# A graph-attention layer on one core: attention dealt out sooner, four overflow slots, five more tiles turned by VectorE

## Chip, cores and metric

One core of a Trainium2 chip runs the whole program. The metric is the device time of one execution in microseconds; the median over the runs counts.

## What is computed

`x` is 2708 × 1024, `adj` 2708 × 2708 with about four ones in a row; all is fp32. Cut to what matters:

```python
h = maximum(layernorm(x), 0)
q = h @ W_q.T + b_q;  k = h @ W_k.T + b_k;  v = h @ W_v.T + b_v
z = scale * (q @ k.T) * adj              # zero entries become -10000
out = x + relu(softmax(z, axis=1) @ v)
```

## The kernel before

Rows are cut into 22 tiles of 128 (the last has 20 rows), sorted by their number of neighbours in two groups, tiles 0 to 7 and from 8 on. `q·k` is computed as `(h·M)·h` with M made from W_q and W_k, so a row's scores are products of its q row with the h rows of its neighbours only. For each tile and each neighbour ("slot") GpSimd gathers 128 rows of h from `h_dram` by an indirect DMA (L610), and VectorE makes one score of 128 rows in one instruction (L863, with the tile's q rows in `pq`). Exponentials and their normalization follow (`weights`, L872 to L911; for the tiles 7 and 20, which have rows without neighbours, L893 to L902), and one weighted sum per slot into `u` (L923, L929). The sums are then multiplied by W_v.

The matrix products go in 20 "units" of two tiles. Units 0 to 9 make q (tiles 0 and 1, 2 and 3, and so on to 18 and 19), units 10 to 19 make the output of two tiles of attention in the order below; the single tile 8 comes last.

```python
order = [6, 5, 4, 3, 2, 0, 20, 7, 17, 13, 18, 12, 19, 11, 15, 10, 14, 1, 16, 9, 8]
```

A unit is a Strassen-Winograd product of seven blocks, each of eight matmul records (L1010): s2, a12, s4, s3, then the first two blocks of the next unit (a11 and s1, `opened`), then a22. The four corners of a unit's result are taken from the banks by c11, c12, c22 and c21; c22 of a late q unit is VectorE's addition at L1091 that reads the bank `psy` directly, into which the last block a22 then accumulates. c21 of a q unit is ScalarE's copy at L1099, after which SP stores the finished q rows (L1084): those of tiles from 8 on into `q_late`. When the attention reaches such a tile, SP loads its rows from `q_late` into `pq` (L833).

A tile's rows must be turned before they are operands. Either TensorE turns eight 128 × 128 pieces through the bank `pt` (L415), or the tile is "faced": ScalarE copies `u` in another order to `v` (L944), stores it in `u_dram`, SP loads it by quarters (`by_quarters`, L700, tile `or`), and VectorE turns 32 × 32 pieces (`faces`, L705). Each unit's operands are made by `upper()` (a11, a12) and `lower()` (a22, s1, s2, s3, s4), called in the unit before at steps 0 and 2. Ten tiles are faced before.

VectorE executes in the order in which the program is written from unit 4 on; the other engines' order is planned. A unit has seven places for VectorE's work, `after(0)` to `after(6)`: s2 comes after `after(1)`, c12 after `after(3)`, c22 after `after(4)`, a22 after `after(5)`. The attention is a generator, `attention(order)`, whose steps are dealt out there: `advance(share)` takes so many steps that their assumed cost, 1.3 us for a score or a sum and 0.6 for weights, comes to the share. The share is 20.9/7, less 2.3/7 for every faced tile of the next unit, from step 2 of unit 5 on.

Two tiles, 0 and 8 (HOSTS), hold the rows with more than 8 neighbours. Slots from 8 on are put into tile 21 (SECOND), whose own 20 rows have no slots: two halves of 64 rows with 7 slots each. Its unnormalized sums go through `v_dram` and are added to the hosts' sums (L929). The attention of SECOND comes just ahead of tile 0.

W_v's four blocks replace M, and their differences replace T, which are M's, while units 9 and 10 run (L1259 loads, L1263 subtractions). Gather buffers are cleared before use, eight of them by VectorE (L1254) while the neighbours are listed and sorted. Results are added to x by an indirect DMA with accumulation on GpSimd (L1109) and put in place by an indirect scatter (L808).

Of the kernel before, what the change touches and what calls it, by code (L numbers as in the profile page):

```python
# [65 lines left out]
def tile_preln_masked_attention(  # L66
# [27 lines left out]
    SECOND = NT - 1  # L94
    HP = P // 2
    VK = K[0] - WIDE
    assert K[0] == K[EARLY] and K[SECOND] == 0 and WIDE + VK <= SLOTS
    for t in HOSTS:
# [66 lines left out]
    msq = const.tile([P, 9 + NT], FT, name="msq")  # L165
    mass = const.tile([P, 2], FT, name="mass")

# [15 lines left out]

    for t in HOSTS:
        nc.vector.memset(cap[:HP, t:t + 1], float(WIDE + VK))
    K[SECOND] = VK
# [122 lines left out]
    def follow(steps):  # L309

        for step in steps.split():
# [11 lines left out]
            elif step[0] in "hk":  # L323
                keep(first, step[0] == "h")
            elif step[0] == "+":
                owe(first)
            elif step[0] == "p":
                counted(first)
            elif step[0] == "c":
                counts(*halves[first])  # L330
            elif step[0] == "o":
                sorted_at.append(sort(*halves[first]))
            elif step[0] == "w":
                pooled.close()
                with tc.issue_after((behind if first < EARLY else products)[-1].ins):
# [298 lines left out]
    def reload(lo, hi):  # L634
# [4 lines left out]
        if hi > FULL:  # L639
            loads.append(nc.gpsimd.dma_start(ptab[:REST, FULL, SLOTS:], src[(FULL - lo) * P:, SLOTS:]))  # L640
        part = slice(HP, P) if lo >= EARLY else slice(0, HP)
        loads.append((nc.gpsimd if lo >= EARLY else nc.sync).dma_start(
            ptab[part, SECOND, 0:SLOTS + 1 - WIDE], src[0:HP, WIDE:SLOTS + 1]))
        for load in loads:
# [170 lines left out]
    def ask(t):  # L815

        g_of[t] = []
        wanted.extend((t, s) for s in range(K[t]))

    def fetch(t):  # L820
# [7 lines left out]
        if t == SECOND:  # L828
            assert EARLY in formed
            gather(tq[t][:HP], q_dram[:, :], t, SLOTS - WIDE, HP)  # L830
            nc.sync.dma_start(tq[t][HP:], q_late[:HP, :])
        elif t >= EARLY:
# [6 lines left out]
    def fill():  # L839
        while wanted and free:  # L840
            t, s = wanted.pop(0)
            g = free.pop(0)
            if s == K[t]:
                half = slice(HOSTS.index(t) * HP, (HOSTS.index(t) + 1) * HP)
                nc.gpsimd.dma_start(g[:HP], v_dram[half, :])
            else:
# [28 lines left out]
    def weights(t):  # L875
# [7 lines left out]
        if t == SECOND:  # L883
            coef = w
            with tc.issue_after(chain[-1].ins):
                chain.append(nc.vector.scalar_tensor_tensor(w[:, :k], w[:, :k], 1.0, ok, op0=ALU.mult, op1=ALU.mult,
                                                            accum_out=mass[:, 0:1]))
            nc.sync.dma_start(mass[:HP, 1:2], mass[HP:, 0:1])
            nc.scalar.activation(u, g_of[t][0], AF.Copy, scale=w[:, 0:1])
# [14 lines left out]
        else:  # L904
            with tc.issue_after(chain[-1].ins):
                nc.vector.scalar_tensor_tensor(w[:, :k], w[:, :k], 1.0, ok, op0=ALU.mult, op1=ALU.mult, accum_out=m[:, 1:2])
                if t in HOSTS:
                    second = HOSTS.index(t)
                    nc.vector.tensor_add(m[:HP, 1:2], m[:HP, 1:2], mass[:HP, second:second + 1])
                nc.vector.reciprocal(m[:, 3:4], m[:, 1:2])  # L910
                chain.append(nc.vector.tensor_scalar(coef[:, :k], w[:, :k], m[:, 3:4], None, op0=ALU.mult))  # L911
            nc.scalar.activation(u, g_of[t][0], AF.Copy, scale=coef[:, 0:1])  # L912
            free.append(g_of[t][0])
            if t in HOSTS:
                assert whole_second
                wanted.insert(0, (t, k))
        us[t] = u, coef, m

    def sums(t):
        u, coef, m = us.pop(t)  # L920
        for s in range(0 if t in EMPTY else 1, K[t]):
            fill()
            chained(lambda: nc.vector.scalar_tensor_tensor(  # L923
                u, g_of[t][s], coef[:, s:s + 1], u, op0=ALU.mult, op1=ALU.add))
            free.append(g_of[t][s])
            yield 1.3
        fill()
        if t in HOSTS:
            chained(lambda: nc.vector.scalar_tensor_tensor(  # L929
                u[:HP], g_of[t][K[t]][:HP], m[:HP, 3:4], u[:HP], op0=ALU.mult, op1=ALU.add))  # L930
            free.append(g_of[t][K[t]])
# [7 lines left out]
        unit = next((n for n, pair in enumerate(units) if pair[0] == "o" and t in pair[1:]), len(units))  # L939
        if now < [unit - 2, 2] and unit <= len(q_pairs) + 4:  # L940
            faced_tiles.add(t)
        if t in faced_tiles:
            v = row_tile(f"v_{t}")
# [15 lines left out]
    def attention(order):  # L959
# [11 lines left out]
        for i, t in enumerate(order):  # L971
            nxt = after[i]
            ahead = nxt is not None and K[t] + K[nxt] <= HIGH + 1
            part = scores(nxt, after[i + 1]) if nxt is not None else iter(())
# [38 lines left out]
    opened_of = {}  # L1013

    def opened(n):

# [6 lines left out]
        nc.scalar.copy(Y, X)  # L1023
        products.append(add_block(Z, ops["s1"], T[:, 0]))
        p5 = small("p5")
# [18 lines left out]
    def multiply(n, results, after):  # L1044
# [6 lines left out]
        after(1)  # L1051
        products.append(add_block(Y, ops["s2"], T[:, 1]))
        u2 = small("u2")
# [57 lines left out]
    def o_results(ta, tb):  # L1111
# [12 lines left out]
        def c12(Z, u2):  # L1124
            nc.vector.tensor_add(u2, Z, u2)
            nc.scalar.activation(ya[:, hi], u2, AF.Relu)
            if ta == NT - 2:

                nc.sync.dma_start(tail_dram, ya[P - 1:, :])
            send(add_x(ya, ta))  # L1130
            sent.append((ya, ta))

        def c21(Y):
            nc.scalar.activation(yb[:, lo], Y, AF.Relu)  # L1134
            send(add_x(yb, tb))
            sent.append((yb, tb))

# [29 lines left out]

    def send(behind):

        while sent:  # L1170
            y, t = sent.pop(0)
            with tc.issue_after(behind.ins):
                scatter(y, t, P)

    def tail(t):
        n = tiles[t][1]
        y = work.tile([P, D], FT, tag="q", name=f"y_{t}", bufs=4)
        nc.sync.dma_start(y[:n], tail_dram.to_broadcast([n, D]))
        add_x(y, t, n)
        scatter(y, t, n)  # L1180

# [7 lines left out]
    alone = order[-1]  # L1189
    units = [("q",) + p for p in q_pairs] + [("o",) + p for p in o_pairs]  # L1190

    def load_rows(unit):
# [17 lines left out]
    products = []  # L1210
    last_q = len(q_pairs) - 1
    summed = []
# [12 lines left out]
    for n, unit in enumerate(units):  # L1225
# [13 lines left out]
        def after(i):  # L1239
            now[1] = i  # L1240
            if (n, i) in steps_ahead:
                follow(steps_ahead[n, i])
            if (n, i) == (2, 5):
                owe(8)
                owe(9)
                rows_of[FIRST] = load_rows(units[FIRST])
                owe(10)
# [3 lines left out]
                pooled.close()  # L1251
            if (n, i) == (FIRST, 1):
                for g in slots[:HIGH - 3]:
                    nc.vector.memset(g, 0.0)  # L1254
# [109 lines left out]
    uT, (X, Z), p1 = single["turned"], single["banks"], single["first"]  # L1364
    add_block(Z, uT[:, 0:4, :], T[:, 0])
    add_block(Z, uT[:, 4:8, :], M[:, 1, 1])
# [188 lines left out]
```

## Time and profile before

| | |
|---|---|
| median of three runs | 641.19 us (641.15 to 641.2) |
| the profiled execution | 639.94 us |
| its span | 638.1 us |
| TensorE, VectorE, ScalarE, GpSimd busy | 98%, 82%, 44%, 56% |
| unit 9's first block starts | 347.10 us |
| the single tile's first block | 611.82 us |

The times of rows count from the span's start. In a timeline row stand the start, the duration, engine, line, operation, output and inputs, and in brackets the idle time before it and what ended it. In a row of the groups stand the count, the busy time, the mean duration in ns, and the idle time before the group's instructions. DMA rows end in the size and the median time to landing.

### The profile page before, as it was taken

The page shows a single profiled execution, that of the slowest core. Times are in us where ns is not written, and L with a number is a line of the kernel's source. Part 1 is how long each engine was busy: PE and PEld are TensorE (multiplying, and loading weights), DVE is VectorE, ACT ScalarE, POOL GpSimd, SP SyncE. Part 2 cuts the span into 40 slices and gives each one's busy share as a digit, 9 for nine tenths or more (in the row PEclk, how much of TensorE's full clock was granted, in tenths as well). Part 3 has the DMA queues.
Part 4 walks back from the last instruction along what each step waited for, and adds up shares of the span by engine and source line. Part 5 has one row for each costly group of instructions (what it writes and reads, how often), then busy time and mean ns, then how long its engine had stood idle before and what let it go on. Part 6 is the DMA issues. An engine that isn't in the chain of part 4 may idle for free.

```text
span 638.1 us, 6156 instructions
## 1 busy us (share of the span) xinstructions
PE 627.8 (98%) x1651; PEld 317.9 (50%) x1651; DVE 522.4 (82%) x1016; ACT 283.6 (44%) x423; POOL 360.2 (56%) x383
## 2 busy tenths in 40 slices
PE   9999999999999999999999999999999999999994
PEld 5777766444444444444444444444444444444441
DVE  5999888997997625999888999999999889989121
ACT  3538985849667533424342144343342432333200
POOL 2639960885768357565651663476466878633311
PEclk9999999999999999999999999999999999999998
DMA  8999997598796439996798998999999999853631
GB/s 335 407 362 321 342 351 286 200 323 330 255 379 231 171 95 317 327 323 223 233 299 289 290 414 222 295 344 311 363 382 325 325 290 291 266 145 77 187 119 50
DMA packets 60192, 176.96 MB, mean 277 GB/s; under 512 B 9799, under 2 KB 15255, under 8 KB 59512
## 3 DMA queue, kind: packets, MB, share of 16 engines
q0 software_dynamic: 25136, 78.41, 39.4%
q1 hardware_dynamic: 29514, 78.61, 35.0%
q10 hardware_dynamic: 5502, 19.48, 7.8%
q8 instruction: 15, 0.25, 0.2%
q14 instruction: 25, 0.20, 0.1%
HBM read 145.65 MB, written 40.74 MB: 292 GB/s over the span
## 4 chain that ended last, share of the span: by engine, by line
PE 90%; issue 4%; POOL 2%; DMA 2%; DVE 1%; POOLq 0%; ACT 0%; ACTq 0%; DVEq 0%
PE ps L1010 40%; PE psy L1010 29%; PE ps_y L476 6%; PE ps_x L476 4%; PE ps_z L476 4%; PE pt L415 4%; POOL g L610 2%; DMA v_dram<-u 1%; DMA M<-h_dram,tab 1%; PE ps_y L511 1%; DVE junk L863 0%; PE ps_h L1218 0%; PE ps_v L594 0%; DVE u L923 0%; DVE s L722 0%
## 5 line engine op out<-in xcount | busy, mean ns | idle before, releaser
L610 POOL DMA_INDIRECT g<-h_dram,tab x94 | 120.2, 1278 | 79.9 <-DVE u L923 30.0
L1010 PE MATMUL psy<-wlow,s 128*128 128x512 f32 x320 | 144.0, 592 | 0.0
L1010 PE MATMUL ps<-M,a 128*128 128x512 f32 x320 | 144.0, 593 | 0.0
L863 DVE SCALAR_TENSOR_TENSOR junk<-g,pq 128x1024 uint8<-128x1024 f32 x93 | 113.8, 1224 | 13.4 <-DMA g<-h_dram,tab 10.4
L1010 PEld LDWEIGHTS ps<-M,a 128*128 128x128 f32 x320 | 59.7, 190 | 70.4 <-issue 69.1
L923 DVE SCALAR_TENSOR_TENSOR u<-g,coef,u 128x1024 f32<-128x1024 f32 x69 | 88.4, 1281 | 7.0 <-ACT u L912 5.8
L1010 PEld LDWEIGHTS psy<-wlow,s 128*128 128x128 f32 x320 | 59.6, 190 | 69.2 <-issue 69.0
L389 DVE FIND_INDEX8 at<-ones,adj 128x8 uint32<-128x685 f32 (+1 forms) x88 | 74.5, 864 | 0.0
L1010 PE MATMUL ps<-wlow,s 128*128 128x512 f32 x160 | 72.0, 593 | 0.4 <-DVE s L722 0.4
L1010 PE MATMUL ps<-M,s 128*128 128x512 f32 x160 | 72.1, 592 | 0.0
L1010 PE MATMUL psy<-wlow,a 128*128 128x512 f32 x160 | 72.0, 593 | 0.0
L368 ACT ACTIVATE sized<-adj 128x2708 uint8<-128x2708 f32 (+1 forms) x22 | 54.3, 2467 | 7.4 <-DMA adj<-in_adj_dram 6.1
L298 POOL TENSOR_TENSOR hsum<-hsum,x 128x256 f32<-128x256 f32 (+1 forms) x56 | 38.6, 732 | 26.2 <-DVE wlow L444 22.5
L1109 POOL DMA_INDIRECT y<-in_x_dram,tab x19 | 34.2, 1798 | 28.9 <-ACT y L1134 12.1
L1010 PEld LDWEIGHTS ps<-wlow,s 128*128 128x128 f32 x160 | 30.3, 190 | 38.9 <-issue 38.5
L1010 PEld LDWEIGHTS psy<-wlow,a 128*128 128x128 f32 x160 | 30.3, 190 | 38.5 <-issue 37.3
L1010 PEld LDWEIGHTS ps<-M,s 128*128 128x128 f32 x160 | 30.3, 190 | 38.1 <-issue 37.4
L808 POOL DMA_INDIRECT out_dram<-y,tab x21 | 27.4, 1306 | 32.0 <-DMA y<-in_x_dram,tab 15.8
L912 ACT ACTIVATE u<-g,coef 128x1024 f32<-128x1024 f32 x18 | 20.7, 1149 | 35.8 <-DVE coef L911 35.6
L276 ACT ACTIVATE x<-x,r 128x1024 f32<-128x1024 f32 (+1 forms) x22 | 25.9, 1232 | 6.6 <-POOL r L266 6.6
L722 DVE TENSOR_TENSOR s<-a,pt 128x512 f32<-128x512 f32 x30 | 19.2, 681 | 10.9 <-ACT a L718 10.9
L476 PE MATMUL ps_y<-wlow 128*128 128x512 f32 x64 | 27.6, 592 | 0.0
(251 smaller groups left out, 843.3 us busy)
## 6 DMA issues: line engine op xcount, KB each, us to landing
adj<-in_adj_dram SPq DMA_DIRECT2D x21, 1354.0 KB, 11.5
x<-in_x_dram SPq DMA_DIRECT2D x21, 512.0 KB, 8.2
h_dram<-x ACTq DMA_DIRECT2D x21, 512.0 KB, 7.4
q_late<-q SPq DMA_DIRECT2D x12, 512.0 KB, 5.1
pq<-q_late SPq DMA_DIRECT2D x12, 512.0 KB, 6.6
u_dram<-v ACTq DMA_DIRECT2D x10, 512.0 KB, 6.4
or<-u_dram SPq DMA_DIRECT2D x40, 128.0 KB, 7.0
M<-in_wv_dram SPq DMA_DIRECT2D x4, 1024.0 KB, 8.4
```

What stands on the lines that cost most here:

```text
L276: nc.scalar.activation(xs[i][:n], xs[i][:n], AF.Relu, bias=r[:n, 4, i:i + 1], scale=r[:n, 3, i:i + 1])
L298: small.append(nc.gpsimd.tensor_add(hsum[:n, cols], hsum[:n, cols], xt[:n, cols]))
L368: nc.scalar.activation(sized[:n], a[:n, :, :PW], AF.Abs, accum_out=total[:n, t:t + 1])
L389: nc.vector.max_index(at[:n, k - first_k, g, :], ones[:n, 0:8], a[:n, g, :])
L415: nc.tensor.transpose(pt[:, c, :], xt[:, k * P:(k + 1) * P], ident)
L476: mm = nc.tensor.matmul(bank, a_tile(o + H * a[0], a[1], i), b(o), start=first and o == 0, stop=(o == H - 1), skip_group_check=True)
L610: return nc.gpsimd.indirect_dma_start(out=dst, out_offset=None, in_=src, in_offset=off, bounds_check=N - 1, oob_is_err=False)
L808: to = nc.gpsimd.indirect_dma_start(out=out, out_offset=bass.IndirectOffsetOnAxis(ap=ptab.bitcast(U32)[:n, t, SLOTS:SLOTS + 1], axis=0), i ...
L863: chained(lambda: nc.vector.scalar_tensor_tensor(junk, g_of[t][s], 1.0, tq[t], op0=ALU.mult, op1=ALU.mult, accum_out=zall[:, t, s:s + 1]))
L923: chained(lambda: nc.vector.scalar_tensor_tensor(u, g_of[t][s], coef[:, s:s + 1], u, op0=ALU.mult, op1=ALU.add))
L1010: mm = nc.tensor.matmul(bank, a[:, c, :], b[:, c, :], start=False, stop=(c == 3), skip_group_check=True)
L1109: return nc.gpsimd.indirect_dma_start(out=y[:n], out_offset=None, in_=x, in_offset=off, compute_op=ALU.add)
```

## The change

- **Overflow.** SECOND has 4 slots in place of 7, and the two hosts' rows are divided over its rows in pieces of 48, 8, 60 and 12; a row with more than 12 neighbours has two pieces. The second piece is added to the first by an accumulating DMA of GpSimd during the host's sums. SECOND stands ahead of tile 3 in place of tile 0.
- **Memsets and sorting.** The eight clearings go to a later place, five on VectorE, three on ScalarE; the search of the table (`searched`) is written one step sooner.
- **Dealing out.** The attention begins at step 0 of unit 5 in place of step 2, with a share of 22.0 in units up to 8, 17.4 in units 9 and 10, and 20.5 after.
- **W_v.** The block b11 and W_v's block 11 are loaded one unit step sooner, the latter into T[:, 0]; b12 − b11 goes into T[:, 1], so these two places are exchanged for the output units (`t_of`). Two subtractions stand one step later.
- **Faced tiles.** Tiles of unit 15 and of units from 19 on are faced too: 18, 12, 16, 9 and the single tile 8, which is finished and loaded at the end of unit 18 and turned in unit 19.
- **Scatters.** Each finished tile is put in place one tile later; the last tile's y lies in another buffer and goes the same way.
- The loads of the first rows of unit 4 stand ahead of two table steps, and the late put of the table waits for other instructions.

```diff
-    HP = P // 2
-    VK = K[0] - WIDE
+    VK = 4
+    OVER = ((48, 0), (8, 48)), ((60, 56), (12, 116))
...
-        wanted.extend((t, s) for s in range(K[t]))
+        wanted.extend((t, s) for s in range(K[t] + (t in HOSTS)))
...
+            if t in HOSTS and s == K[t] // 2 + 1:
+                assert len(g_of[t]) == K[t] + 1
+                rows, at = OVER[HOSTS.index(t)][1]
+                nc.gpsimd.dma_start(g_of[t][K[t]][:rows], v_dram[at:at + rows, :], accum_op=ALU.add)
...
-        if now < [unit - 2, 2] and unit <= len(q_pairs) + 4:
+        if now < [unit - 2, 2] and unit <= len(q_pairs) + 5 or unit >= len(units) - 1:
             faced_tiles.add(t)
...
-    stream = attention(order[:order.index(0)] + [SECOND] + order[order.index(0):])
+    stream = attention(order[:order.index(3)] + [SECOND] + order[order.index(3):])
...
+    def t_of(n, k):
+        return T[:, (1, 0, 2, 3)[k] if n > last_q else k]
...
-            send(add_x(ya, ta))
-            sent.append((ya, ta))
+            send(add_x(ya, ta), 1)
+            sent.append((ya, ta, P))
...
-    def send(behind):
-        while sent:
-            y, t = sent.pop(0)
+    def send(behind, stay=0):
+        while len(sent) > stay:
             with tc.issue_after(behind.ins):
-                scatter(y, t, P)
+                scatter(*sent.pop(0))
...
-        share = 20.9 / 7
+        share = (22.0 if n < last_q else 17.4 if n < last_q + 2 else 20.5) / 7
...
-            if (n, i) == (FIRST, 1):
-                for g in slots[:HIGH - 3]:
-                    nc.vector.memset(g, 0.0)
...
-            for at, place, src in (((-1, 0), b12, of_wv(0, 1)), ((0, 0), b11, of_wv(0, 0)), ((0, 2), T[:, 1], of_wv(1, 1)),
+            for at, place, src in (((-1, 0), b12, of_wv(0, 1)), ((-1, 6), b11, of_wv(0, 0)), ((-1, 6), T[:, 0], of_wv(1, 1)),
                                    ((0, 3), b21, of_wv(1, 0)), ((0, 4), b22, of_wv(1, 1))):
...
-            for at, place, a, b in (((0, 2), T[:, 0], b12, b11), ((0, 4), T[:, 1], T[:, 1], T[:, 0]),
-                                    ((1, 0), T[:, 2], b22, b12), ((1, 1), T[:, 3], b21, T[:, 1])):
+            for at, place, a, b in (((0, 2), T[:, 1], b12, b11), ((0, 4), T[:, 0], T[:, 0], T[:, 1]),
+                                    ((1, 1), T[:, 2], b22, b12), ((1, 2), T[:, 3], b21, T[:, 0])):
...
-            if n > FIRST + 1 or n == FIRST + 1 and i > 1:
+            if n > FIRST:
                 advance(share)
...
+            if (n, i) == (3, 5):
+                for g in slots[5:8]:
+                    nc.scalar.activation(g.rearrange("p (a b) -> p a b", b=P), ones.unsqueeze(1).to_broadcast([P, DC, P]),
+                                         AF.Copy, scale=0.0)
...
-            if (n, i) == (3, 4):
+            if (n, i) == (3, 3):
                 searched()
+            if (n, i) in ((3, 3), (3, 4)):
+                for g in slots[:2] if i == 3 else slots[2:5]:
+                    nc.vector.memset(g, 0.0)
...
             if nxt is None and i == 1:
+                uT = work.tile([P, D], FT, tag="hT", name="T_alone", bufs=2).rearrange("p (c q) -> p c q", q=P)
+                faces(uT, single["rows"], 0, DC)
+                single["turned"] = uT
+            if n == len(units) - 2 and i == 6:
                 while alone not in done:
                     advance(1.0)
-                r, = load_rows(("o", alone))
-                single["turned"] = turned(r, "alone")
+                single["rows"], = load_rows(("o", alone))
```

`FIRST` is 4, `EARLY` 8, `HIGH` 11, `last_q` 9, `len(q_pairs)` 10; `(n, i)` is a step i of unit n.

More of the change, by code (lines that the diff above doesn't have):

```diff
@@ L94, in tile_preln_masked_attention @@
     SECOND = NT - 1
-    HP = P // 2
-    VK = K[0] - WIDE
-    assert K[0] == K[EARLY] and K[SECOND] == 0 and WIDE + VK <= SLOTS
+    VK = 4
+    OVER = ((48, 0), (8, 48)), ((60, 56), (12, 116))
+    assert K[0] == K[EARLY] <= WIDE + 2 * VK == SLOTS and K[SECOND] == 0
+    assert sum(rows for host in OVER for rows, at in host) == P
     for t in HOSTS:
@@ L165, in tile_preln_masked_attention @@
     msq = const.tile([P, 9 + NT], FT, name="msq")
-    mass = const.tile([P, 2], FT, name="mass")
+    mass = const.tile([P, 4], FT, name="mass")
+    nc.vector.memset(mass, 0.0)
     nc.vector.tensor_copy(past, rows_i)
@@ L182, in tile_preln_masked_attention @@
         t = e
-    for t in HOSTS:
-        nc.vector.memset(cap[:HP, t:t + 1], float(WIDE + VK))
+    for t, parts in zip(HOSTS, OVER):
+        for i, (rows, at) in enumerate(parts):
+            nc.vector.memset(cap[:rows, t:t + 1], float(WIDE + (i + 1) * VK))
     K[SECOND] = VK
@@ L334, in follow @@
                 pooled.close()
-                with tc.issue_after((behind if first < EARLY else products)[-1].ins):
+                with tc.issue_after((behind if first < EARLY else rooted if first > EARLY else products)[-1].ins):
                     entered.append(put(first, int(last[0]) + 1))
@@ L640, in reload @@
             loads.append(nc.gpsimd.dma_start(ptab[:REST, FULL, SLOTS:], src[(FULL - lo) * P:, SLOTS:]))
-        part = slice(HP, P) if lo >= EARLY else slice(0, HP)
-        loads.append((nc.gpsimd if lo >= EARLY else nc.sync).dma_start(
-            ptab[part, SECOND, 0:SLOTS + 1 - WIDE], src[0:HP, WIDE:SLOTS + 1]))
+        for i, (rows, at) in enumerate(OVER[lo >= EARLY]):
+            slot = WIDE + i * VK
+            loads.append((nc.gpsimd if lo >= EARLY else nc.sync).dma_start(
+                ptab[at:at + rows, SECOND, 0:SLOTS + 1 - slot], src[0:rows, slot:SLOTS + 1]))
+            if i and lo < EARLY:
+                loads.append(nc.sync.dma_start(ptab[at:at + rows, SECOND, SLOTS - WIDE:SLOTS + 1 - WIDE],
+                                               src[0:rows, SLOTS:SLOTS + 1]))
         for load in loads:
@@ L829, in fetch @@
             assert EARLY in formed
-            gather(tq[t][:HP], q_dram[:, :], t, SLOTS - WIDE, HP)
-            nc.sync.dma_start(tq[t][HP:], q_late[:HP, :])
+            rows = sum(rows for rows, at in OVER[0])
+            gather(tq[t][:rows], q_dram[:, :], t, SLOTS - WIDE, rows)
+            for rows, at in OVER[1]:
+                nc.sync.dma_start(tq[t][at:at + rows], q_late[:rows, :])
         elif t >= EARLY:
@@ L843, in fill @@
             if s == K[t]:
-                half = slice(HOSTS.index(t) * HP, (HOSTS.index(t) + 1) * HP)
-                nc.gpsimd.dma_start(g[:HP], v_dram[half, :])
+                assert whole_second
+                rows, at = OVER[HOSTS.index(t)][0]
+                nc.gpsimd.dma_start(g[:rows], v_dram[at:at + rows, :])
             else:
@@ L907, in weights @@
                 if t in HOSTS:
-                    second = HOSTS.index(t)
-                    nc.vector.tensor_add(m[:HP, 1:2], m[:HP, 1:2], mass[:HP, second:second + 1])
+                    c, rows = HOSTS.index(t), OVER[HOSTS.index(t)][0][0]
+                    nc.vector.scalar_tensor_tensor(m[:rows, 1:2], m[:rows, 1:2], mass[:rows, c:c + 1],
+                                                   mass[:rows, c + 2:c + 3], op0=ALU.add, op1=ALU.add)
                 nc.vector.reciprocal(m[:, 3:4], m[:, 1:2])
@@ L928, in sums @@
         if t in HOSTS:
+            rows = OVER[HOSTS.index(t)][0][0]
             chained(lambda: nc.vector.scalar_tensor_tensor(
-                u[:HP], g_of[t][K[t]][:HP], m[:HP, 3:4], u[:HP], op0=ALU.mult, op1=ALU.add))
+                u[:rows], g_of[t][K[t]][:rows], m[:rows, 3:4], u[:rows], op0=ALU.mult, op1=ALU.add))
             free.append(g_of[t][K[t]])
@@ L972, in attention @@
             nxt = after[i]
-            ahead = nxt is not None and K[t] + K[nxt] <= HIGH + 1
+            ahead = nxt is not None and K[t] + (t in HOSTS) + K[nxt] <= HIGH + 1
             part = scores(nxt, after[i + 1]) if nxt is not None else iter(())
```

25 lines of the change are left out of this document (12 added, 13 removed).

## The prediction

> **What bounds the kernel now.** I read the page first: the span, the busy time of each engine and the shares of the chain that ended last. The execution took 639.94 us, its span 638.1, and the median of the three runs is 641.19; I sum on the execution and add 1.25 at the end.
>
> ```profile
> span 638.1 us, 6156 instructions
> PE 627.8 (98%) x1651; PEld 317.9 (50%) x1651; DVE 522.4 (82%) x1016; ACT 283.6 (44%) x423; POOL 360.2 (56%) x383
> PE 90%; issue 4%; POOL 2%; DMA 2%; DVE 1%; POOLq 0%; ACT 0%; ACTq 0%; DVEq 0%
> ```
>
> TensorE is busy 98% and carries 90% of the chain. Whatever leaves TensorE's work is a gain, and every moment TensorE stands still is a loss; a saving on another engine counts only if it prevents such a moment. The chain in order of time shows what a turned tile costs there.
>
> ```profile
> 472.76 0.87 PE pt L415 x8
> 473.63 6.87 PE ps L1010 x16
> ```
>
> Eight turns take 0.87 us of the chain, and sixteen product records 6.87: a block of eight is 3.43, a unit of seven blocks 24.0. Next, where TensorE waits already (timeline and waits; what stands in brackets is idle time before the row and who ended it):
>
> ```profile
> 367.06 0.68 DVE L1091 TENSOR_TENSOR q<-psy,p 128x512 f32<-128x512 f32 x1
> 367.66 1.27 DVE L923 SCALAR_TENSOR_TENSOR u<-g,coef,u 128x1024 f32<-128x1024 f32 x1
> 367.79 0.30 PEld L1010 LDWEIGHTS psy<-wlow,a 128*128 128x128 f32 x2 [0.76 <-DVE q L1091]
> 367.80 3.70 PE L1010 MATMUL psy<-wlow,a 128*128 128x512 f32 x8
> 389.03 3.67 PE L1010 MATMUL ps<-wlow,s 128*128 128x512 f32 x8 [0.36 <-DVE s L722]
> ```
>
> Both times VectorE is the last to come. At 367.8, near the end of unit 9 (the last q pair), TensorE's last block may only start when VectorE has taken the corner c22 out of the bank it accumulates in (L1091). Without that it would have started about 0.1 earlier, at 367.7. So VectorE, which executes in the written order, is just in time there, and anything that holds it up ahead of c22 of unit 9 stops TensorE at once. Small stalls today: 0.1 + 0.36 = 0.46.
>
> **The change: faced tiles.** Five more tiles (18, 12, 16, 9 and the single tile 8) are turned by VectorE. This removes 5 × 0.87 = 4.36 us from TensorE's path (8 × 109 ns each, five times). VectorE gains faces and loses nothing on its path, as the late units have idle time on it; ScalarE gains a copy and a store, SP the loads by quarters.
>
> The Trainium skill speaks against this edit (VectorE: DVE Perf Modes, sections on the three transpose paths and rules for authors): it gives TensorE 390 ns for a 128×128 turn in bf16 and says VectorE transposes only 32×32 blocks. By its 390 ns the five tiles would give 40 × 0.39 = 15.6 us and the total would be 638; the chain's 0.87 for eight in this kernel decides.
>
> Covers of the faced tiles, at nothing:
>
> ```profile
> u_dram<-v ACTq DMA_DIRECT2D x10, 512.0 KB, 6.4
> or<-u_dram SPq DMA_DIRECT2D x40, 128.0 KB, 7.0
> 586.70 1.28 DVE L929 SCALAR_TENSOR_TENSOR u<-g,m,u 64x1024 f32<-64x1024 f32 x1
> 611.82 3.60 PE L1010 MATMUL ps<-M,T_alone 128*128 128x512 f32 x8
> ```
>
> Store and load need 6.4 + 7.0, the copy some 1 to 2, the first faces 1.4: 16 to 17. Tiles 18 and 12 are finished by unit 12's first steps and their loads are written at step 4 of unit 13, tiles 16 and 9 a full unit before their first face: 20 or more each. The single tile ends at 588.0 and is used at 611.8, 24 later, so 7 are left. Without that cover each us too late would be a us of TensorE.
>
> **Four slots, memsets, scatters.** The overflow tile has 4 slots in place of 7: three scores and three sums fewer.
>
> ```profile
> L863 DVE SCALAR_TENSOR_TENSOR junk<-g,pq 128x1024 uint8<-128x1024 f32 x93 | 113.8, 1224 | 13.4 <-DMA g<-h_dram,tab 10.4
> L923 DVE SCALAR_TENSOR_TENSOR u<-g,coef,u 128x1024 f32<-128x1024 f32 x69 | 88.4, 1281 | 7.0 <-ACT u L912 5.8
> L1254 DVE MEMSET g<- 128x1024 f32 x8 | 7.3, 912 | 1.3 <-issue 1.1 <-DVE q L1094 0.2
> 235.20 0.98 POOL L612 DMA_INDIRECT pq<-q_dram,tab  x1 [4.45 <-DMA tab<-tab_dram]
> 245.75 0.95 POOL L612 DMA_INDIRECT pq<-q_dram,tab  x1 [0.30 <-issue]
> 253.19 1.22 DVE L863 SCALAR_TENSOR_TENSOR junk<-g,pq 128x1024 uint8<-128x1024 f32 x1 [1.02 <-DMA pq<-q_dram,tab]
> ```
>
> 3 × 1.224 + 3 × 1.281 = 7.5 us of VectorE, off the path. The extra small loads on SP and the accumulating transfer on GpSimd for rows of the two long tiles go with other waiting and I put them at nothing (0 to 4 us of VectorE, hidden beneath the wait found below). The eight memsets stand among the candidate listing now; half of their 7.3 us lies ahead of the index table on which GpSimd waits (235.20). Moved, and three of them given to ScalarE, the table comes about 3.7 earlier (bounds 0 and 7.3), and with it the second tile's q rows: VectorE's score of 253.19 waits for the gather of 245.75, so 3.5 earlier there too. The later scatters cost nothing: they sit on GpSimd and the last ones follow the end as before. W_v's blocks are exchanged in place and subtracted a step later; VectorE does the same four subtractions, and TensorE does not wait for them today.
>
> **Attention begins sooner and is dealt out faster: the term that decides.** Units 5 to 8 now give out 28 calls × 22/7 = 88 us of attention, against 26 × 20.9/7 = 77.6, and the overflow tile is 7.5 shorter. I went through the written order call by call. Tile 17's first score stands at step 1 of unit 10 before, and at step 0 of unit 9 after. But tile 17's q row is made by unit 8:
>
> ```profile
> 347.10 3.60 PE L1010 MATMUL psy<-wlow,s 128*128 128x512 f32 x8
> 347.66 0.57 ACT L1099 COPY q<-psy 128x512 f32<-128x512 f32 x1
> 348.25 0.33 SPq L1084 DMA_DIRECT2D q_late<-q  x1
> q_late<-q SPq DMA_DIRECT2D x12, 512.0 KB, 5.1
> pq<-q_late SPq DMA_DIRECT2D x12, 512.0 KB, 6.6
> DMA to landing us min/median/max: 3.1/5.7/11.6
> DMA to landing us min/median/max: 4.6/6.6/9.3
> 381.55 1.23 DVE L863 SCALAR_TENSOR_TENSOR junk<-g,pq 128x1024 uint8<-128x1024 f32 x1 [0.20 <-DMA pq<-q_late]
> ```
>
> Unit 8's last block ends at 347.1; ScalarE takes the last corner; SP stores the row at 348.25 and must load it again as pq of tile 17. Of the two ranges the first is of the stores, the second of the loads. With 5.1 and 6.6 the row lands at 360.0, with SP's own issue 360.2 (355.9 to 369.2 by the extremes). VectorE gets there sooner: 381.4 today, less the work that now comes behind this score (four W_v subtractions 9.1, three sides of operands, each of two faces and two operations, 8.3, c12 and c22 1.4, the bias subtraction 0.7), less 7.5 and 3.5 from above: 351. So it waits some 9 us, in order, and behind this score are written, up to c22 of unit 9: four scores (three of tile 17, one of 13), both sides of operands of unit 10 (four faces, four operations), the bias subtraction, two W_v subtractions, the weights of tile 7, its two sums, c12 and c22.
>
> ```profile
> L705 DVE STREAM_TRANSPOSE a<-or 128x512 f32<-128x512 f32 x15 | 10.0, 694 | 1.0 <-DMA or<-u_dram 1.0
> L722 DVE TENSOR_TENSOR s<-a,pt 128x512 f32<-128x512 f32 x30 | 19.2, 681 | 10.9 <-ACT a L718 10.9
> L1263 DVE TENSOR_TENSOR wlow<-M 128x2048 f32<-128x2048 f32 x2 | 4.6, 2282 | 0.0
> 371.34 0.14 DVE L894 TENSOR_SCALAR coef<-keys 128x1 f32<-128x1 f32 x1
> 373.27 0.15 DVE L902 TENSOR_TENSOR m<-w,m 128x1 f32<-128x1 f32 x1
> ```
>
> 4 × 1.224 + 4 × 0.694 + 4 × 0.681 + 0.68 + 2 × 2.282 + 2.1 (such weights, first to last row) + 2 × 1.281 + 2 × 0.68 = 21.7. Rows in a queue overlap by 0.08 (367.06 + 0.68 against 367.66), nineteen times 1.5: 20.2. The last block of unit 9 then starts at 360.2 + 20.2 = 380.4 in place of 367.7: TensorE stands still for 12.7 us (8.4 by the shortest transfers, 21.7 by the longest; I take the medians, which are many alike). It is not given back, as TensorE is the bound again afterwards. Tile 18's q row, from unit 9, meets its score in the same way one unit later, but VectorE has some 17 us written ahead of that score: 0.5 (0 to 8).
>
> By a rule of the Trainium skill (DMA: Bandwidth & Descriptors, anatomy of one DMA), about 2.0 us plus bytes over 436 GB/s, each of the two transfers would take an estimated 3.2 us, tile 17 would land at 355 and the total would be 644. The page fits that to another kind of issue; the rows here say 5.1 and 6.6.
>
> Sum: 639.94 − 4.36 − 0.46 + 12.7 + 0.5 = 648.3; with 1.25, 649.6.
>
> **Rivals.** *Same side, worse.* The attention's start doesn't move, as something other than the memsets holds the table (GpSimd's 4.45 at 235.20 is a wait for a transfer). Then VectorE runs up to 3.5 behind in units 6 to 8, whose c22 also frees TensorE's bank, and tile 17's row is made later by that: 649.6 + 3.5 = 653. For it: 10 us more work is dealt to these units. Against: the memsets do stand in the way.
> *Only a lag.* The row of tile 17 does not hold VectorE, because the score stands where the row has landed already or is fetched in another way than I read. Then VectorE at 351 needs 20.2 to c22, 371.2, and TensorE stalls 3.5: 641.19 − 4.36 − 0.46 + 3.5 = 639.9.
> *No stall.* It ends on the other side. Tile 17's first score falls behind c22 of unit 9, as it does before. From its place at step 0 to c22 there are six steps of attention; as 64 are given out in units 5 to 8, my count would have to be some six too many. Then six steps and the weights, 9.5 us, leave the queue ahead of c22, VectorE is there at 371.2 − 9.5 = 361.7, ahead of TensorE's 367.7, and the row has landed before it is wanted: 641.19 − 4.36 − 0.46 = 636.4. For it: unit 9's share is cut to 17.4 less 4.6 for its two faced tiles, and VectorE has 7.5 us less to do. Against: 5 of 7 calls of 1.83 before c22 still leave the score well ahead of it, and the q row is only stored at 348.25.
> *Not as told.* The loads of the new faced tiles come late and the turns' 4.36 go into waiting: 641.
>
> **How the numbers follow.** About 0.2%, 1.3 us, is what a measurement here can tell from no change. Forecast 0.61; worse 0.14; only a lag 0.06 (a third each faster, the same, slower); no stall 0.17; not as told 0.02 (the same). Faster 0.17 + 0.02 = 0.19; same 0.02 + 0.02 = 0.04; slower 0.61 + 0.14 + 0.02 = 0.77. The forecast's own range is 645 to 658. The range leaves out the no-stall case and the longest transfers: 639 to 657.
>
> **What would show it.** In the profile after: 15 faced tiles and 40 turns fewer; VectorE's first score near 238; a score with about 9 us of waiting for pq from q_late near 351 to 360; behind it a load of TensorE's weights of some 12 us waiting for VectorE's L1091, once. If pq waits but TensorE doesn't, my list of what is queued is wrong; if TensorE has no gap over 1 us, the whole forecast is.

## The result and the profile after

| | before | after |
|---|---|---|
| median | 641.15 us (640.8 to 641.2, 5 runs) | 655.68 us (652.93 to 656.05, 5 runs) |
| profiled execution | 639.94 us | 652.93 us |
| its span | 638.1 us | 651.0 us |

The ratio is 1.0219, with a 95% interval of 1.02 to 1.0237: slower by 2.2%. The profiled execution is the shortest of the five, so the accounts below are of 13.0 us, 639.94 to 652.93.

The page of the kernel after, the lines that answer to the first ones of the prediction:

```profile
span 651.0 us, 6123 instructions
PE 627.7 (96%) x1611; PEld 314.3 (48%) x1611; DVE 519.1 (80%) x1016; ACT 287.0 (44%) x423; POOL 361.8 (56%) x383
PE 40%; DVE 6%; issue 5%; DMA 5%; POOL 2%; ACT 1%; SPq 0%; POOLq 0%; DVEq 0%; ACTq 0%
```

The 40 turns are gone (1611 against 1651 matmuls), yet TensorE is busy as long as before: its records have become longer, as some were executed slowly after a stop. The shares of the chain can't be set beside those of before: they add up to 59%, as the chain could be followed back from the end only to 262.29 us. So I go by TensorE's waits. By cause, us in total, times, longest:

```profile
PE ps L1025 <- DVE s L729: 4.3, 1, 4.3
PE ps L1025 <- DVE a L712: 3.5, 1, 3.5
PE pt L418 <- DMA qr<-h_dram,tab: 2.2, 2, 1.6
...
PE psy L1025 <- DVE q L1109: 1.2, 1, 1.2
PE psy L1025 <- ACT u L1072: 0.8, 1, 0.8
PE ps L1025 <- ACT p L1044: 0.7, 1, 0.7
PE psy L1025 <- ACT taken L1093: 0.3, 1, 0.3
```

And its loads of weights for c22, in the same form:

```profile
PEld psy L1025 <- DVE q L1109: 2.2, 2, 2.0
```

Where the time is lost, the timeline tells. In the kernel after, unit 9's first block and unit 10's fourth (s3) start at

```profile
352.96 3.60 PE L1025 MATMUL psy<-wlow,s 128*128 128x512 f32 x8
399.64 3.60 PE L1025 MATMUL psy<-wlow,s 128*128 128x512 f32 x8
```

and in the kernel before unit 9 starts at 347.10 and that fourth block at

```profile
381.63 3.60 PE L1010 MATMUL psy<-wlow,s 128*128 128x512 f32 x8
```

Unit 9 begins 352.96 − 347.10 = 5.9 us late. At s3 of unit 10 the delay is 399.64 − 381.63 = 18.0, so units 9 and 10 lose 12.1. The end is 651.0 − 638.1 = 12.9 late, so 5.1 are won after that, where the five tiles are no longer turned. 5.9 + 12.1 − 5.1 = 12.9.

VectorE's and SP's rows around unit 9, in the kernel after:

```profile
355.03 0.33 SPq L1102 DMA_DIRECT2D q_late<-q  x1
364.69 1.01 SPq L842 DMA_DIRECT2D pq<-q_late  x2
368.42 1.22 DVE L873 SCALAR_TENSOR_TENSOR junk<-g,pq 128x1024 uint8<-128x1024 f32 x1 [14.98 <-DMA pq<-q_late]
372.51 2.28 DVE L1277 TENSOR_TENSOR wlow<-M 128x2048 f32<-128x2048 f32 x1
388.05 0.69 DVE L1109 TENSOR_TENSOR q<-psy,p 128x512 f32<-128x512 f32 x1
```

This is the forecast wait of VectorE. It stands still for 15.0 us at tile 17's first score, from 353.4. Its q row is stored at 355.03, loaded from 364.69 and there at 368.4. From the score's start to the end of c22 (L1109, 388.74) are 20.3 us of queued work. And TensorE behind it:

```profile
370.34 5.10 PE L1025 MATMUL ps<-M,a 128*128 128x512 f32 x8 [3.48 <-DVE a L712]
379.76 5.37 PE L1025 MATMUL ps<-wlow,s 128*128 128x512 f32 x8 [4.33 <-DVE s L729]
385.81 2.84 PE L1025 MATMUL ps<-M,s 128*128 128x512 f32 x6 [0.68 <-ACT p L1044]
391.06 3.60 PE L1025 MATMUL psy<-wlow,a 128*128 128x512 f32 x8
```

And two windows of 10 us there (length, then PE, PEld, DVE, ACT and POOL busy with their records, the granted clock, the DMA share, GB/s):

```profile
366.00:376.00 10.00, 5.96 (x10) 2.03 (x9) 7.02 (x15) 0.98 (x3) 0.00 (x0) 0.83 0.99 353
376.00:386.00 10.00, 5.56 (x9) 2.20 (x10) 9.82 (x15) 2.18 (x4) 2.56 (x2) 0.83 0.32 66
```

Unit 10's first two blocks (a11 and s1) wait for its operands, which stand behind the score: 3.48 + 4.33 idle, and a 0.68 follows. These two blocks take 5.10 and 5.37 in place of 3.60, with a granted clock of 0.83 in both windows: 1.5 and 1.8 more. Together 11.8 of the 12.1. The last block of unit 9 (a22, 391.06) has no wait before it: when c22 was out at 388.74, TensorE was busy with twelve records of unit 10 (385.81 to 391.06).

### The profile page after: what moved, and what is told of

Read it like the earlier page. It is cut to its first block, busy times and chain, and to the rows that moved or that the text cites. A ratio compares the mean times of both kernels' runs of the same rounds, so it can differ in the third digit from the quotient of the medians.

```text
span 651.0 us, 6123 instructions
## 1 busy us (share of the span) xinstructions
PE 627.7 (96%) x1611; PEld 314.3 (48%) x1611; DVE 519.1 (80%) x1016; ACT 287.0 (44%) x423; POOL 361.8 (56%) x383
## 4 chain that ended last, share of the span: by engine, by line
PE 40%; DVE 6%; issue 5%; DMA 5%; POOL 2%; ACT 1%; SPq 0%; POOLq 0%; DVEq 0%; ACTq 0%
PE ps L1025 23%; PE psy L1025 16%; DVE u L936 3%; DMA q_late<-q 2%; DVE junk L873 1%; DMA or<-u_dram 1%; DMA g<-h_dram,tab 1%; POOL g L613 1%; DVE s L729 1%; PE pt L418 1%; POOL qr L615 0%; ACT u L924 0%; DVE q L1112 0%; DVE u L943 0%; ACT u L914 0%
## 5 line engine op out<-in xcount | busy, mean ns | idle before, releaser
L1025 PE MATMUL ps<-M,a 128*128 128x512 f32 x320 | 145.8, 598 | 3.5 <-DVE a L712 3.5
L873 DVE SCALAR_TENSOR_TENSOR junk<-g,pq 128x1024 uint8<-128x1024 f32 x92 | 112.4, 1222 | 38.8 <-DMA g<-h_dram,tab 16.6
L936 DVE SCALAR_TENSOR_TENSOR u<-g,coef,u 128x1024 f32<-128x1024 f32 x71 | 91.0, 1281 | 7.6 <-ACT u L924 6.2
L1025 PE MATMUL ps<-wlow,s 128*128 128x512 f32 x160 | 73.7, 604 | 4.3 <-DVE s L729 4.3
L959 ACT COPY v<-u 128x1024 f32<-128x1024 f32 x15 | 15.7, 1046 | 47.9 <-DVE u L936 35.6
L815 POOL DMA_INDIRECT out_dram<-y,tab x21 | 25.2, 1202 | 17.5 <-DMA y<-in_x_dram,tab 9.3
L924 ACT ACTIVATE u<-g,coef 128x1024 f32<-128x1024 f32 x18 | 20.7, 1147 | 25.6 <-DVE coef L923 19.1
L767 ACT COPY ps<-bp_sb 128x512 f32<-128x512 f32 x42 | 24.6, 597 | 16.4 <-DVE bp_sb L1345 11.6
```

Of the source, the lines that this page charges most:

```text
L767: nc.scalar.copy(return_[h], row[:, h * NB:(h + 1) * NB])
L815: to = nc.gpsimd.indirect_dma_start(out=out, out_offset=bass.IndirectOffsetOnAxis(ap=ptab.bitcast(U32)[:n, t, SLOTS:SLOTS + 1], axis=0), i ...
L873: chained(lambda: nc.vector.scalar_tensor_tensor(junk, g_of[t][s], 1.0, tq[t], op0=ALU.mult, op1=ALU.mult, accum_out=zall[:, t, s:s + 1]))
L936: chained(lambda: nc.vector.scalar_tensor_tensor(u, g_of[t][s], coef[:, s:s + 1], u, op0=ALU.mult, op1=ALU.add))
L1025: mm = nc.tensor.matmul(bank, a[:, c, :], b[:, c, :], start=False, stop=(c == 3), skip_group_check=True)
```

## The experiments

Theory A: the stop at units 9 and 10 is the wait for tile 17's q row. Theory B: VectorE has too much ahead of c22 of unit 9, whatever it waits for. The experiments of one group (1 to 4; 5 to 8; 9 and 10; 11 and 12) share a chip and the runs of the kernel before on it, to which each ratio refers; across groups only the ratios compare. A `print` of the kernel after is left out of the experiments made from it, so their lines behind it have a number lower by one.

**1. Another tile at the critical place.** The kernel after, with

```diff
-    order = [6, 5, 4, 3, 2, 0, 20, 7, 17, 13, 18,
+    order = [6, 5, 4, 3, 2, 0, 20, 7, 13, 17, 18,
```

> The changed kernel with tiles 17 and 13 exchanged in the attention's order, so that the score that is dealt at step 0 of unit 9 belongs to tile 13, whose q row was stored two units sooner. The dealing, the shares and the number of instructions stay. Theory A (the 12 us stop of TensorE at units 9 and 10 is the wait for tile 17's q row): the wait of 15.0 us on VectorE goes, c22 of unit 9 comes at about 373.7, when TensorE wants it, and the time falls by 11 to 12 us, to 641 to 645. Theory B (too much VectorE work is dealt ahead of c22 of unit 9, and the wait for the row only takes up time that would be lost anyway): it falls by less than 4 us.

Measured: 643.95 us against 640.28 before, ratio 1.0056 (1.0037 to 1.0074) in place of 1.0219: by the ratios 1.6%, some 10.4 us, less than the kernel after. VectorE has no wait for `q_late` left, and TensorE none from unit 9 on. From unit 9's first block to s3 of unit 10, the first two rows below, are 34.3 us, against 34.5 before and 46.7 after: the whole 12.1 is gone. Theory A holds, B falls: with the same dealing c22 comes in time. What is left stands ahead of unit 9, which begins 8.6 late here (timeline of TensorE, ScalarE and GpSimd):

```profile
355.69 3.60 PE L1024 MATMUL psy<-wlow,s 128*128 128x512 f32 x8
390.02 3.60 PE L1024 MATMUL psy<-wlow,s 128*128 128x512 f32 x8
255.77 1.15 ACT L924 ACTIVATE u<-g,coef 128x1024 f32<-128x1024 f32 x1 [7.67 <-issue]
256.83 0.56 ACT L1071 COPY u<-psy 128x512 f32<-128x512 f32 x1
257.45 2.84 PE L1024 MATMUL psy<-wlow,s 128*128 128x512 f32 x6 [2.26 <-ACT u L1071]
321.06 3.70 PE L1024 MATMUL psy<-wlow,a 128*128 128x512 f32 x8 [0.52 <-DVE q L1108]
323.36 0.98 POOL L615 DMA_INDIRECT qr<-h_dram,tab  x1 [0.30 <-issue]
325.32 1.06 PE L418 MATMUL pt<-ident,qr 128*128 128x128 f32 x8 [0.56 <-DMA qr<-h_dram,tab]
332.47 1.06 PE L418 MATMUL pt<-ident,qr 128*128 128x128 f32 x8 [2.65 <-DMA qr<-h_dram,tab]
```

ScalarE's copy of a bank (L1071) is queued behind the attention's L924, which stands still with VectorE until the second tile's q rows are there. And GpSimd gathers the last q unit's rows at 323.36, between gathers for the attention; in the kernel before it was at 309.65.

**2. The dealing of before in the kernel after.**

```diff
-        share = (22.0 if n < last_q else 17.4 if n < last_q + 2 else 20.5) / 7
+        share = 20.9 / 7
...
-            if n > FIRST:
+            if n > FIRST + 1 or n == FIRST + 1 and i > 1:
```

> The changed kernel with the dealing of before: share 20.9 everywhere, from step 2 of unit 5. Tile 17's first score then stands right behind c22 of unit 9, and less attention is dealt in units 5 to 8. Theory A: the stop at units 9 and 10 goes (12 us), and the 5.5 us of small stops in units 5 to 8, if they too come from the dealing, shrink: 636 to 639, faster than before by the turned tiles. Theory B: with the dealing of before the lag goes as well, also about 637; a third theory, that the exchanged W_v blocks or the overflow's new transfers hold VectorE, leaves 645 or more.

Measured: 646.2 us, ratio 1.0092 (1.0063 to 1.0122). The stops ahead of unit 9 are gone, but VectorE's wait for the row is not, against what theories A and B foresaw. The time is that of the third theory (645 or more), but its cause isn't: VectorE waits here neither for W_v's blocks nor for the overflow's transfers.

```profile
375.75 1.23 DVE L873 SCALAR_TENSOR_TENSOR junk<-g,pq 128x1024 uint8<-128x1024 f32 x1 [7.17 <-DMA pq<-q_late]
387.34 6.14 PE L1024 MATMUL psy<-wlow,s 128*128 128x512 f32 x8 [4.70 <-DVE wlow L1276]
```

The score now comes behind c22 (367.90), and what it holds up is a subtraction of W_v's blocks, which unit 10 wants: 4.70 idle and 2.5 of slow records. So with the dealing of before the row still costs TensorE 7.2 us; the rest of the change, too, moves the score forward. Three smaller stops follow near 550 and 620.

**3. The five tiles alone,** in the kernel before: the conditions of `faced_tiles` and the lines of the single tile as in the diff.

> The kernel before with the five more faced tiles alone (tiles 18, 12, 16, 9 and the single tile 8). The recorded step, 5 x 0.87 us off TensorE's path with the transfers covered: 4.4 us less than before, 636.4 to 637.2. Rival: the copies, stores and loads by quarters come late and TensorE waits: no gain, or up to 4 us slower.

Measured: 646.08 us, ratio 1.0078 (1.0055 to 1.0101): slower by some 5 us, where 4.4 less was expected. My cover for the single tile was wrong there, and a second stop stands at 492:

```profile
492.28 5.16 PE L1010 MATMUL psy<-wlow,a 128*128 128x512 f32 x8 [2.95 <-ACT taken L1075]
598.12 1.28 DVE L929 SCALAR_TENSOR_TENSOR u<-g,m,u 64x1024 f32<-64x1024 f32 x1
615.18 1.25 DVE L705 STREAM_TRANSPOSE T_alone<-or 128x1024 f32<-128x1024 f32 x1 [14.72 <-DMA or<-u_dram]
616.48 6.20 PE L1010 MATMUL ps<-M,T_alone 128*128 128x512 f32 x8 [3.92 <-DVE T_alone L705]
```

The single tile's sums end at 599.4, not at 588.0 as before. By the code more faced tiles take from the share (2.3/7 each), so that the attention ends later; no run tried this alone. From there to the use 17.1 us pass, as I had estimated, and TensorE is there 3.9 sooner. In the kernel after, the attention has 7.5 us less to do and TensorE comes 13 later, and TensorE does not wait for the same tile.

**4. The new dealing alone,** in the kernel before: the lines of the second experiment the other way.

> The kernel before with the new shares (22.0, 17.4, 20.5) and the start at step 0 of unit 5 alone. With seven overflow slots tile 17's first score stands at step 4 of unit 9, just ahead of c22. Theory A: little is queued between it and c22, so TensorE loses 0 to 3 us there, not 12; the small stops of units 5 to 8 (5.5 us in the changed kernel), if the dealing makes them, are here too: 642 to 649. Theory B: VectorE has more ahead of c22 than in the changed kernel (7.5 us of overflow), so the loss is 12 us or more: above 653.

Measured: 655.08 us, ratio 1.0238 (1.0215 to 1.0262). The dealing alone makes a loss as large as the whole change's, and more than theory A foresaw for a score so near to c22. The profile has several waits one after another; the first two rows are unit 9's first block and unit 10's last:

```profile
353.93 3.60 PE L1010 MATMUL psy<-wlow,s 128*128 128x512 f32 x8
406.90 3.60 PE L1010 MATMUL psy<-wlow,a 128*128 128x512 f32 x8
257.42 2.93 PE L1010 MATMUL psy<-wlow,s 128*128 128x512 f32 x3 [3.32 <-ACT u L1054]
274.83 1.06 PE L415 MATMUL pt<-ident,qr 128*128 128x128 f32 x8 [2.01 <-DMA qr<-h_dram,tab]
365.37 2.29 DVE L1263 TENSOR_TENSOR wlow<-M 128x2048 f32<-128x2048 f32 x1 [4.93 <-DMA M<-in_wv_dram]
378.68 5.37 PE L1010 MATMUL psy<-wlow,s 128*128 128x512 f32 x8 [3.99 <-DVE wlow L1263]
384.85 1.23 DVE L863 SCALAR_TENSOR_TENSOR junk<-g,pq 128x1024 uint8<-128x1024 f32 x1 [5.12 <-DMA pq<-q_late]
```

The stops of 257 and of the rows to be turned are here too, so the dealing makes them. By its number this run speaks for theory B; by its rows it shows transfers that VectorE arrives at too soon. Unit 9 begins 6.8 late. Unit 10's last block, at 392.54 before, is 14.4 late, so units 9 and 10 lose 7.5: 4.0 idle and 1.8 of slow records behind the load of W_v's first block (VectorE's 4.9), and smaller waits. TensorE doesn't wait for c22, and the row is not what holds it first.

**5. The start of the dealing,** on the first experiment's kernel:

```diff
-            if n > FIRST:
+            if n > FIRST + 1 or n == FIRST + 1 and i > 1:
```

> The changed kernel with 17 and 13 exchanged, as in the first experiment, and the dealing begun at step 2 of unit 5 as before, the new shares kept. In the first experiment TensorE still lost some 8 us before unit 9: about 3 near 257 us, where ScalarE's copy of a bank is queued behind the first weighted slot of the attention, which waits for VectorE, and VectorE for the second tile's q rows; the rest between 321 and 333, where rows to be turned are gathered late on GpSimd. Theory C (both come from the start two steps earlier while the first q rows land only 1.0 us earlier): all of it goes, 636 to 637.5. Theory D (the larger share makes GpSimd's queue late): only the first goes, 640 to 641.

Measured: 638.25 us against 640.33, ratio 0.9963 (0.995 to 0.9976): 0.4% faster than the kernel before, a little over the 636 to 637.5 of theory C. Theory C holds all the same: TensorE has no stop ahead of unit 9. One is left, and it is W_v's:

```profile
348.06 0.38 SPq L1272 DMA_DIRECT2D M<-in_wv_dram  x1
359.16 2.29 DVE L1276 TENSOR_TENSOR wlow<-M 128x2048 f32<-128x2048 f32 x1 [7.74 <-DMA M<-in_wv_dram]
366.40 5.32 PE L1024 MATMUL ps<-wlow,s 128*128 128x512 f32 x8 [2.25 <-DVE s L729]
```

The load of W_v's first block, written sooner by the change, is executed at 348.06 (340.43 in the kernel before): the planned order puts it behind the store of tile 17's q row on SP (347.62).

**6. And the shares.** The fifth with `share = 20.9 / 7`.

> As the last, and with the share of 20.9 everywhere as well: the second experiment with 17 and 13 exchanged. Theory A: the 7.2 us wait of VectorE for tile 17's q row, and TensorE's 4.7 us with its slow restart of 2.5, go: 646.2 - 7 = 639; what is left are waits near 550 and 620 that only this dealing showed. If the wait for the row was not the cause there, 645 or more.

Measured: 639.51 us, ratio 0.9982 (0.9971 to 0.9993). Against the second experiment the exchange of the two tiles gives 1.1%, 7 us, as A has it; the small stops stay.

**7. Ten faced tiles** on the first experiment's kernel.

> The first experiment's kernel with the ten faced tiles of before instead of 15: the five tiles are turned by TensorE again. The recorded step: they are worth 5 x 0.87 = 4.4 us as long as their cover holds, so this is 4.4 us slower than the first experiment, 648 to 649. Rival, after the third experiment, in which the five tiles alone gained nothing since waits took their place near 492 and 616: no difference, 642 to 645.

Measured: 647.2 us, ratio 1.0114 (1.0087 to 1.0142), against 1.0056 with 15: 0.58%, 3.7 us, about 1.6 to 5.8 with both intervals taken together. In the two profiles unit 9 begins at the same time (355.67 and 355.69), and the spans differ by 4.4 (645.8 and 641.4). The step holds where its cover does.

**8. The exchange of 17 and 13 in the kernel before.**

> The kernel before with 17 and 13 exchanged and nothing else. There the wait for the row was 0.2 us, so theory A gives no change, 640 to 641. If the exchange has a merit of its own (other transfers, another order of the output pairs), it shows here as a gain of some us.

Measured: 641.83 us, ratio 1.0025 (1.001 to 1.004). The exchange has no merit of its own; it is a little slower, with a turned tile late by 1.8 at 471.

**9. A subtraction one step later,** on the fifth's kernel: `((0, 2), T[:, 1], b12, b11)` becomes `((0, 3), ...)`.

> The fifth experiment's kernel with the subtraction b12 - b11 one step later (step 3 of unit 9 in place of 2). There VectorE waited 7.7 us at 359 for the load of W_v's first block, ahead of unit 10's lower operands, and TensorE lost 2.3 us at 366 and 1.7 in the restart. With the operands first, the load lands while VectorE makes them: 638.25 - 4 = 634.3. If the operands are late for another reason, or the later subtraction itself holds s1 of unit 10 or c22 of unit 9, no gain: 638 or more.

Measured: 639.96 us beside a reference of 644.74 for the kernel before on this chip, ratio 0.9948 (0.9922 to 0.9975). TensorE's wait of 2.3 is gone from the profile, and VectorE's 7.7 for W_v's block is 2.3 now; a wait of TensorE for c22 is left:

```profile
369.51 3.70 PE L1024 MATMUL psy<-wlow,a 128*128 128x512 f32 x8 [1.72 <-DVE q L1108]
```

The 4 us expected over the fifth aren't shown: its interval overlaps the fifth's.

**10. The later start without the exchange.** The kernel after, with the edit of the fifth alone.

> The changed kernel with the start of the dealing at step 2 of unit 5 and nothing else: 17 stays ahead of 13. Tile 17's first score then stands at step 4 of unit 9, right ahead of c22. Theory A with C: the 8 us before unit 9 go; the score finds its row at about 362 and c22 follows within 2 us, but the subtraction and the scores behind it are late for unit 10: TensorE loses 0 to 7 us, 637 to 645. Theory A without C: 648 or more.

Measured: 645.16 us, ratio 1.0017 (0.9992 to 1.0042). One condition of the change, put back, takes 2% of the time away (ratio 1.0219 to 1.0017). What is left is again the row, which VectorE gets at 379.8 and not at about 362 as expected:

```profile
355.02 16.83 SPq L707 DMA_DIRECT2D or<-u_dram  x8
372.20 0.34 SPq L842 DMA_DIRECT2D pq<-q_late  x1
379.77 1.23 DVE L873 SCALAR_TENSOR_TENSOR junk<-g,pq 128x1024 uint8<-128x1024 f32 x1 [7.46 <-DMA pq<-q_late]
382.93 5.40 PE L1024 MATMUL psy<-wlow,a 128*128 128x512 f32 x8 [4.29 <-DVE q L1108]
```

The reason is another one here. The row was stored at 348.34, but its load is issued only at 372.20, as eight loads by quarters stand ahead of it on SP. And here TensorE does stop at c22, as the prediction had it.

**11 and 12. A smaller share in unit 9** (14.0, on the ninth's kernel), **and the fifth once more** beside it.

> The ninth experiment's kernel with a share of 14.0 in unit 9 in place of 17.4. In the ninth, c22 of unit 9 still comes 1.7 us late for TensorE, behind two scores of tile 13; with the smaller share these scores fall behind c22. If that is all, 1.7 us less than the ninth experiment (ratio to before 0.992). If the attention given away there is missed later (tiles 18, 12 and 8 are finished later, and their transfers lose their cover), as in the third experiment, no gain or a loss, with waits near 490 or at the single tile.

> The fifth experiment's kernel once more, beside the last, as the ninth ran beside another reference: its ratio to the kernel before was 0.9963, and with the 1.7 us of the c22 and the 4 us of the late subtraction against it, it should stand 0.5 to 1% above the eleventh experiment if those waits count, and level with it if they are taken up elsewhere.

Measured: 638.82 us, ratio 0.9973 (0.9945 to 1.0), and 638.51 us, 0.9971 (0.9957 to 0.9984). Level, where 0.5 to 1% was expected if the waits count: the two further edits, the later subtraction and the smaller share, are worth nothing that could be told. In the eleventh c22 is 2.6 late, behind a wait of 4.3 for W_v's block, and the single tile 0.8; in this execution of the fifth's kernel VectorE waits 5.7 us for that block, and TensorE only 0.2 behind it.

## Why the prediction was right, and where its sizes were off

The forecast was 649.6 us, slower; measured were 655.68. In the profiled execution's frame it was 648.3 against 652.93. The 4.6 between them are the 5.9 ahead of unit 9, which the sum lacks, less some small differences of the other terms.

- *The term that decides: right in its cause, wrong in its path.* VectorE waits for tile 17's row, and all that is written behind the score is late; experiments 1 and 6 show this cause, and experiment 8 that the exchange has no merit of its own. VectorE was at the score at 353.4 (forecast 351), and 20.3 us were queued up to the end of c22 (20.2). The wait was 15.0 in place of 9: unit 8 ended 5.9 later, so the row was stored at 355.03 and not at 348.25, and it took 13.4 from there in place of 11.7 + 0.2, the store alone 9.5, within the trace's 3.1 to 11.6.
- *The step that failed: where TensorE stops.* I had it stop once, for 12.7, at the last block of unit 9, which waits for c22. In the profile the weights of that block don't wait for c22; the longest such wait is 2.0, ahead of unit 9. I had listed unit 10's operands as work ahead of c22 and overlooked that a11 and s1 of unit 10, which TensorE executes before that last block, need them. TensorE stopped there: 8.5 us idle, with the 0.68 behind, and 3.3 of slow records, a term that the forecast did not have. c22 itself came 15.2 late, at 388.74 against 373.6 (367.7 and unit 9's 5.9), and its delay was partly filled by the twelve records of unit 10. So 12.7 against 12.1 is in part luck.
- *Mis-sized: the start.* "The table comes about 3.7 earlier" was 1.0: the first score stands at 240.98, against 241.99. The second tile's, forecast 3.5 earlier, is 2.5 earlier (250.66 against 253.19). The memsets did leave the listing, but the sort then waited for TensorE, on which its first product stood behind a whole block:

```profile
216.50 0.23 PE L685 MATMUL ps_in<-sort,before 128*128 128x144 bf16 x1
216.82 0.31 DVE L689 COPY sort<-ps_all 128x144 f32<-128x144 f32 x1 [2.06 <-PE ps_all L687]
```

- *Missing: 5.9 us ahead of unit 9.* This is the rival "same side, worse" in its place, and I gave it 0.14 and 3.5 us. Its condition came about for the most part, as the first score moved by 1.0 alone, but its mechanism only in the smaller part: I weighed only VectorE's c22, and that cost 1.2 of idle time. The rest came over other engines' queues: ScalarE's L924 in front of a copy (0.8), GpSimd's gathers in front of the rows to be turned (0.6 and 1.6), and the restart after each. I had followed the moved steps on VectorE's queue alone. Experiments 5 and 10, which differ from 1 and from the kernel after only in the start at step 0, show that this start makes these stops.
- *Faced tiles.* Forecast −4.36. After unit 10 the kernel wins 5.1, which with the two old stalls (0.36 of the 0.46 lies there) leaves some 4.7; experiment 7 has 3.7, with 1.6 to 5.8 as its interval. The cover of the single tile held in the kernel after, but I had read it from the kernel before, where it doesn't hold (experiment 3).
- *Costed at nothing.* The wait for W_v's first block is not there in the kernel after, as VectorE is late anyway, nor in experiments 1, 2 and 6. It is there in 5, 7 and 9 to 12, and in 4 too, which has W_v's loads as before; so the exchange of W_v's places isn't shown to be its cause. "Tile 18: 0.5" was 0: VectorE waits for `q_late` once.
- *From the profile to the median.* I added 1.25; the profiled execution was the fastest of five, 2.75 under the median.

Shown is that the 12.1 are the wait for tile 17's row, and that the 5.9 come from the start at step 0. That the dealing alone brings the score too far forward is not shown: in experiment 2, with the dealing of before, the row still costs 7.2. Which part of the rest moves it (the shorter overflow, by 7.5 us of VectorE, is the likely one) stays open, as do the overflow, the scatters and the memsets by themselves, since no run has one of them alone.

## What to carry to other kernels

When work is dealt out sooner, take each item that is dealt and ask when its input is made: here one row of scores was moved ahead of the end of its own store and load, and everything written behind it in order paid. Ask too which of the bound engine's next blocks is the first to need something of that queue; it may be an earlier one than the one that waits today. Follow each moved step on all queues it enters, since small copies and gathers that feed the bound engine sit there too. A saving on the bound engine is only as good as the slack of what replaces it, and that slack must be read after all other edits, not in the kernel before.

## What the runs showed of the hardware

A stop of TensorE can cost more than its idle time: after 3.5 and 4.3 us the next eight records took 5.10 and 5.37 us in place of 3.60, with a granted clock of 0.83 in those windows. After 1.17 us (the kernel after, at 319.36) they took 3.70. The length of the stop alone does not decide: after 2.26 us in experiment 1 (257.45) eight records took 3.70, after 2.25 us in experiment 5 (366.40) 5.32. The store of tile 17's row, 512 KB, took 9.5 us from issue to landing here, where the median before was 5.1. The runs of the kernel after scatter by 3.1 us, those of before beside them by 0.4; but beside experiment 9 the kernel before scattered by 6.2 too, so that the scatter comes from the transfers on the path isn't shown.
